# An attention block over 64 sequence pairs on one core: the third pair's keys' product moved between the first pair's probability transposes, a bias fold moved ahead of a turned x1, more warming transposes

## The chip, the cores and the metric

The kernel runs on one core of a Trainium2 chip. The metric is the device time of one execution in microseconds (us), here 1495.01 (median of three runs, 1494.42 to 1495.22). Five engines run side by side, each through a queue of its own in program order: TensorE (PE in the profile; PEld is its weight load) multiplies and transposes into PSUM, VectorE (DVE), ScalarE (ACT) and GpSimd (POOL) do elementwise work and reductions, SyncE (SP) and ScalarE issue transfers. They meet through semaphores.

## The reference

One transformer block with cross attention, float32, over 128 sequences of 128 positions and 256 features, 16 heads of 16 features, and a hidden layer of 1024:

```python
q = (query @ Wq + bq).reshape(b, s, N_HEADS, D_K).transpose(0, 2, 1, 3)
k = (key @ Wk + bk)...
v = (values @ Wv + bv)...
scores = jnp.einsum('bhqd,bhkd->bhqk', q, k) / jnp.sqrt(jnp.float32(D_K))
scores = jnp.where(j < i + mask, scores, NEG_INF)
attn = jax.nn.softmax(scores, axis=-1)
attn = attn.at[:, :, 0, :].set(0.0)
ctx = jnp.einsum('bhqk,bhkd->bhqd', attn, v)...
attn_out = ctx @ Wo + bo
x = layer_norm(query + attn_out, ln1_g, ln1_b)
ffn = jax.nn.relu(x @ W1 + b1) @ W2 + b2
out = layer_norm(x + ffn, ln2_g, ln2_b)
```

Here `mask` is 0 and `key` and `values` are the same context tensor, so that each position sees strictly earlier ones, and position 0 sees none.

## The kernel before

The 128 sequences are taken as 64 pairs (`p`); every function below works on one pair. A pair goes through: `tokens` (its rows, transposed on DVE), `queries`, `keys` and `values` (products on TensorE, copied out of PSUM by ACT), `scores` (TensorE; `hi=1` is the high half of the rows, which sees all 128 columns, `hi=0` the low half, which sees 64), `mask` and `maximum` (DVE, then a subtraction on POOL), `exponential` (ACT), `sums` (DVE, then a division on POOL), a transposition of the probabilities, `weigh` (probabilities by values), `context` (ACT copy), `attention_out`, `attention_sum`, `attention_stats` and `shift` (DVE and POOL), `norm1` (x1), a transposition of x1, `hidden` (first layer, with ACT's ReLU), `second`, the second norm, `store`.

Tile's scheduling is switched off (`manual_schedule`), so the order of the calls is the order of each engine's queue. Pairs 0 to 6 have hand-written orders (the opening in the body, then `third`, `fourth`, `fifth`, `fall_in`, `sixth`); from pair 7 on `step(p)` repeats. In one stage several pairs are under way: `third` takes pair 2 through its scores while pair 0 goes through its first layer and pair 1 through its probabilities.

PSUM is eight banks. Scores use banks 0 to 3. In the opening everything else takes banks 4 to 7 in turn: `bank(name)` raises a counter and returns `4 + turns[0] % 4`. A product may be written to a bank only when the last reader of what it held is done; later stages name fixed banks.

Probabilities of pairs 0 and 1, and x1 of pair 0, are transposed on TensorE (`turn_on_pe`, L493, four 128x128 transposes and an ACT copy for each group; `turn_x1_on_pe`, L710, with ACT's scale and bias at L720). From pair 2 on DVE transposes 32x32 blocks (`turn`, L468) and 16 transfers reorder them (`bring`, L481, from SP's and ACT's queues); x1 takes the same way through DRAM (`turn_x1`, L699: four transfers out at L241, one back at L244).

`keys` is `project_keys` (TensorE, L263) and `copy_keys` (ACT, four copies at L293). `values` is TensorE's product (L303); `values_out` has ACT copy it into two layouts (L317, L326). `fold_values` makes a row that `add_values` (L695) copies to where `add_bo` (POOL, L256) reads it.

`fold_norm1` (L653) multiplies the first norm's bias with W1 on TensorE (L660) and has ACT copy four rows out (L668); `add_b1` (L670) sends them to a column by four transfers. The column is used from pair 1 on.

The program starts with 12 transposes of the identity (L995) whose result nobody reads, before the first context rows have arrived. `hidden` for pair 1 (L738) has empty instructions on TensorE between its products (`empty`, L215): six behind each product of its first group, three behind each of the rest. In the trace each float32 product or projection shows as two instructions.

`load_ahead` and `load_tokens` issue the transfers for later pairs on SP's queue; a transfer may wait for an earlier one of the same semaphore, of which eight are used in turn.

## Time and profile before

| what | us |
| --- | --- |
| median of the runs shown | 1495.01 |
| the profiled execution, whole | 1494.63 |
| its span, first to last instruction | 1492.9 |
| TensorE busy | 1478.8 |
| DVE busy | 1379.4 |
| POOL busy | 1359.7 |
| ACT busy | 1321.3 |

Of the 40 slices of the span, the one that holds the first 37 us has TensorE at eight tenths, all others but the last at nine or more. A row of the timeline has the start in us from the span's beginning, the time that the group took, engine, line, operation, out<-in, shape and count, and in brackets how long the engine had been idle before it and what ended that. Rows of neighbouring instructions of one form are merged, so the time of a group on TensorE includes the drain of its last product; start to start is the better measure there. A matmul's end is modelled.

### The profile page before, as it was taken

Reading aid. Unit: us, or ns where it says so; the run is one execution under the profiler, and the core shown is the slowest. Engines: PE = TensorE matmul, PEld = TensorE weight load, DVE = VectorE, ACT = ScalarE, POOL = GpSimd, SP = SyncE. Lnnn points to the kernel's source line nnn. Section 1 sums busy time; section 2 is a strip of 40 time slices with the busy share of each in tenths; the row PEclk is TensorE's granted clock in tenths of the full one; section 3 lists DMA queues with packets and bytes.
Section 4 is the critical chain, followed back from the end, with each engine's and each line's share of the span. In section 5 each row is a group of like instructions: output and inputs, shape, how many; then the busy total and the mean of one; then the engine's idle time right before and its main releaser. Section 6 shows DMA issues by size and latency. Waiting matters only on the chain.

```text
span 1492.9 us, 53293 instructions
## 1 busy us (share of the span) xinstructions
PE 1478.8 (99%) x19270; PEld 1376.9 (92%) x19270; DVE 1379.4 (92%) x2428; ACT 1321.3 (89%) x5271; POOL 1359.7 (91%) x1510
## 2 busy tenths in 40 slices
PE   8999999999999999999999999999999999999998
PEld 6778999999999999999999999999999999999997
DVE  6989999999999999999999999999999999999965
ACT  5658999999999999999999999999999999999962
POOL 6878899999999999999999999999999999999983
PEclk9999999999999999999999999999999999999999
DMA  9356666566566566556656665666665666664451
GB/s 200 85 109 147 146 146 137 139 143 140 147 139 144 136 141 143 141 132 147 145 135 147 146 136 140 144 138 150 140 143 138 139 140 147 133 143 132 108 126 49
DMA packets 415314, 204.59 MB, mean 137 GB/s; under 512 B 282448, under 2 KB 383056, under 8 KB 415056
## 3 DMA queue, kind: packets, MB, share of 16 engines
q1 hardware_dynamic: 412768, 199.34, 57.5%
q8 instruction: 158, 2.59, 0.8%
q10 hardware_dynamic: 2288, 1.85, 0.5%
q14 instruction: 100, 0.82, 0.2%
HBM read 70.26 MB, written 33.29 MB: 69 GB/s over the span
## 4 chain that ended last, share of the span: by engine, by line
PE 89%; DVE 4%; ACT 3%; POOL 2%; issue 1%; DMA 1%; ACTq 0%; SPq 0%; POOLq 0%; DVEq 0%
PE banks L835 24%; PE banks L933 23%; PE banks L263 14%; PE banks L550 7%; PE banks L303 7%; PE banks L387 6%; PE banks L531 3%; PE banks L521 2%; PE banks L738 2%; ACT sm L800 1%; DVE su L445 1%; PE banks L758 0%; ACT hT L746 0%; DVE sm L411 0%; DVE tb L474 0%
## 5 line engine op out<-in xcount | busy, mean ns | idle before, releaser
L800 ACT ACTIVATE sm<-banks,nmx 128x128 f32<-128x128 f32 x944 | 329.0, 377 | 20.9 <-DVE nmx L784 11.2
L462 POOL TENSOR_TENSOR sm<-sm,rs 128x1024 f32<-128x1024 f32 x171 | 322.3, 1899 | 0.9 <-DVE rs L457 0.9
L800 ACT ACTIVATE sm<-sm,nmx 128x64 f32<-128x64 f32 x944 | 312.3, 365 | 0.0
L474 DVE STREAM_TRANSPOSE tb<-sm 128x1024 f32<-128x1024 f32 x186 | 229.4, 1236 | 12.0 <-DMA pT<-tb 6.9
L964 ACT ACTIVATE hT<-hT,b1e_c 128x256 f32<-128x256 f32 x448 | 191.3, 497 | 28.8 <-DVE hT L952 22.8
L800 ACT ACTIVATION_READ_ACCUMULATOR sm<-sm,nmx 128x1 f32 x912 | 198.9, 218 | 0.0
L800 ACT ACTIVATION_READ_ACCUMULATOR sm<-banks,nmx 128x1 f32 x912 | 197.8, 217 | 0.0
L835 PE MATMUL banks<-wt,hS 128*128 128x128 f32 x1440 | 170.7, 275 | 0.1
L933 PE MATMUL banks<-xS,w1t 128*128 128x128 f32 x1344 | 168.4, 275 | 0.0
L835 PEld LDWEIGHTS banks<-wt,hS 128*128 128x128 f32 x1440 | 165.6, 192 | 0.3 <-DVE hS L820 0.3
L784 DVE TENSOR_REDUCE nmx<-banks 128x4 f32<-128x512 f32 x177 | 153.8, 869 | 6.0
L933 PEld LDWEIGHTS banks<-xS,w1t 128*128 128x128 f32 x1344 | 159.1, 192 | 0.0
L293 ACT ACTIVATE kT<-banks,bkh,half 128x256 f32<-128x256 f32 x252 | 122.0, 584 | 4.0 <-PE banks L263 4.0
L263 PE MATMUL banks<-xT,wq 128*128 128x256 f32 x504 | 125.4, 392 | 0.0
L550 PE MATMUL banks<-wo,cxT 128*128 128x256 f32 x512 | 121.3, 380 | 0.8 <-ACT cxT L543 0.8
L303 PE MATMUL banks<-wv,cT 128*128 128x256 f32 x512 | 120.9, 379 | 0.0
L835 PEld LDWEIGHTS banks<-w,hT 128*128 128x128 f32 x960 | 116.6, 192 | 3.5 <-ACT cxT L543 0.3
L263 PE MATMUL banks<-cT,wk 128*128 128x256 f32 x504 | 119.2, 379 | 0.0
L933 PE MATMUL banks<-x1T,w 128*128 128x128 f32 x896 | 118.3, 275 | 0.0
L835 PE MATMUL banks<-w,hT 128*128 128x128 f32 x960 | 117.5, 275 | 0.1
L550 PEld LDWEIGHTS banks<-wo,cxT 128*128 128x128 f32 x512 | 96.9, 190 | 14.5 <-ACT cxT L543 1.3
L303 PEld LDWEIGHTS banks<-wv,cT 128*128 128x128 f32 x512 | 97.2, 190 | 13.2
(160 smaller groups left out, 3958.4 us busy)
## 6 DMA issues: line engine op xcount, KB each, us to landing
pT<-tb SPq DMA_DIRECT2D x976, 96.0 KB, 2.2
x1t<-tbx SPq DMA_DIRECT2D x252, 64.0 KB, 1.8
x1T<-x1t SPq DMA_DIRECT2D x63, 256.0 KB, 3.0
out_dram<-t SPq DMA_DIRECT2D x63, 256.0 KB, 2.4
xb<-in_x_dram SPq DMA_DIRECT2D x124, 128.0 KB, 4.1
cb<-in_ctx_dram SPq DMA_DIRECT2D x124, 128.0 KB, 3.8
x<-in_x_dram SPq DMA_DIRECT2D x31, 512.0 KB, 4.7
w<-in_L_xattn_W_dram SPq DMA_DIRECT2D x2, 1024.0 KB, 8.2
```

The source lines that it names most:

```text
L263: nc.tensor.matmul(ps[:, m * TP : (m + 1) * TP], w[:, k, m * P : (m + 1) * P], src[:, k, :], start=(k == 0), stop=(k == KC - 1),)
L293: nc.scalar.activation(st["kT"][:, m, e, :], pk[:, m * TP : (m + 1) * TP], AF.Identity, bias=bkh[:, m, e : e + 1], scale=half[:, e : e + 1],)
L303: nc.tensor.matmul(pv[:, s * D : (s + 1) * D], st["cT"][:, k, s * P : (s + 1) * P], wv[:, k, :], start=(k == 0), stop=(k == KC - 1),)
L387: nc.tensor.matmul(st["sps", hi][r][s * HP : (s + 1) * HP, m * 2 * n : (m + 1) * 2 * n].rearrange("p (e j) -> p e j", e=2), st["qT"][strip ...
L462: nc.gpsimd.tensor_tensor(sm[:, part, :], sm[:, part, :], st["rs", hi][:, part, None].to_broadcast([P, part.stop - part.start, sm.shape[2] ...
L474: nc.vector.transpose(st["tb"][:, :, at : at + 256].rearrange("p j (n a) -> p n j a", a=32), st["sm", hi].rearrange("p h j -> p (h j)")[:, ...
L550: nc.tensor.matmul(po[:, s * D : (s + 1) * D], cxT[:, k, s, :], wo[:, k, :], start=(k == 0), stop=(k == KC - 1),)
L784: nc.vector.tensor_reduce(st["nmx", 1][:, 4 * first : 4 * (first + n)], ps, AX.X, ALU.max, negate=True,)
L800: nc.scalar.activation(sm[:, h, :], src, AF.Exp, bias=nmx[:, h : h + 1], scale=1.0, **({"accum_out": st["su", hi][:, h : h + 1]} if summed ...
L835: nc.tensor.matmul(out, left(k), right(k), start=(k == 0), stop=(k == FC // 2 - 1))
L933: nc.tensor.matmul(ps[:, i * P : (i + 1) * P].rearrange("p (n a) -> p n a", a=32), left(i), right, start=True, stop=True,)
L964: nc.scalar.activation(self.hT[:, f], self.plains.get(f, self.hT[:, f]), AF.Relu, bias=b1e_c[:, f : f + 1], scale=1.0,)
```

## The change

The diff touches the opening only; the repeated `step` stays as it is.

```diff
+    def next_bank(i):
+        turns[0] = (i - 5) % 4
...
                     if p == 1:
-                        empty(3 if f else 6)
+                        empty(2)
...
-    for i in range(12):
-        nc.tensor.transpose(warm[:, i % 4 * P : (i % 4 + 1) * P], ident, ident)
+
+    def keep_warm(n):
+        for i in range(n):
+            nc.tensor.transpose(warm[:, i % 4 * P : (i % 4 + 1) * P], ident, ident)
+
+    keep_warm(16)
     states[0] = {}
...
         nc.vector.tensor_copy(st[which + "T"].rearrange("p k i -> p (k i)"), pt)
+    keep_warm(3)
...
     ps_bv = fold_values()
+    add_values(ps_bv)
+    tokens(2, "c")
     sums(0, 0, ALL)
     scores(1, 1)
     mask(1, 1, A)
     maximum(1, 1, ONE)
+    values_out(1)
     turn_on_pe(0, 1, range(2))
-    add_values(ps_bv)
-    values_out(1)
-    turn_on_pe(0, 1, range(2, 4))
+    next_bank(6)
+    project_keys(2)
+    next_bank(5)
+    turn_on_pe(0, 1, range(2, 3))
+    next_bank(7)
+    turn_on_pe(0, 1, range(3, 4))
     mask(1, 1, B)
     maximum(1, 1, TWO)
     add_bo(0)
+    next_bank(4)
     turn_on_pe(0, 0, range(2))
     tokens(2, "x")
     scores(1, 0)
     exponential(1, 1, ONE)
+    next_bank(7)
     weigh(0)
...
     maximum(1, 0, ALL)
-    tokens(2, "c")
     exponential(1, 1, TWO)
...
     shift(0, 1)
+    copy_keys(2)
     exponential(1, 0, ALL)
     sums(1, 1, TWO)
-    keys(2)
     norm1(0)
     sums(1, 0, ALL)
     nc.gpsimd.tensor_tensor(be1b_r, be1_r, b2_r, ALU.add)
+    next_bank(7)
     values(2)
...
         maximum(p, 1, ONE)
+        fold_norm1()
+        add_b1()
         turn_x1_on_pe(0)
         turn_on_pe(1, 1, range(2))
-        fold_norm1()
-        add_b1()
         hidden(0, range(FC // 4))
...
         tokens(3, "c")
-        load_ahead(2)
-        load_tokens(2)
         exponential(p, 0, ALL)
...
         hidden(0, range(3 * FC // 4, FC), lambda f: bring(p, nc.scalar, EVERY[8:]))
+        load_ahead(2)
+        load_tokens(2)
```

In words, with pairs counted from 0: the first warming run has 16 transposes, and three more follow the transposes of the first tokens. ACT copies the folded row and pair 1's values before the first copies of pair 0's turned probabilities. DVE transposes pair 2's context before pair 0's low sums, TensorE makes pair 2's key product between the second and third group of pair 0's high half, and ACT copies these keys before pair 1's low Exp. `next_bank(i)` makes the next `bank` return bank i, so that the rotation fits the new order. In `third`, the bias fold and its four transfers stand before the transposes of pair 0's x1. The loads of pairs 6 and 7 and of the third group of tokens are issued at the end of `third`, behind pair 2's reordering transfers and pair 1's x1. The empty instructions in pair 1's first layer become two behind each product.

## The prediction

> **What bounds the kernel now.** I read the page first, then TensorE's waits over the first 130 us, then the timeline of that stretch engine by engine.

> ```profile
> span 1492.9 us, 53293 instructions
> ...
> PE 1478.8 (99%) x19270; PEld 1376.9 (92%) x19270; DVE 1379.4 (92%) x2428; ACT 1321.3 (89%) x5271; POOL 1359.7 (91%) x1510
> ```

> TensorE is busy throughout. Its waits in the first 130 us (engine, line, releaser: total, times, longest) are:

> ```profile
> PE banks L504 <- ACT vd L326: 2.3, 1, 2.3
> ...
> PE banks L738 <- DMA x1T<-x1t: 0.6, 1, 0.6
> PE banks L387 <- ACT hT L746: 0.6, 1, 0.6
> ```

> From 160 us on the same view has no entry. So the loop over pairs runs at TensorE's pace, and whatever the opening gains or loses by about 95 us is carried to the end one for one. All edits lie in that opening; the sum is the shift of TensorE's timeline there.

> **1. The warming transposes.** TensorE's timeline (start, us, line, count):

> ```profile
> 1.44 2.82 PE L995 MATMUL banks<-ident 128*128 128x128 f32 x12 [1.44 <-POOL ident masks.py:199]
> 4.97 1.12 PE L230 MATMUL banks<-ident,c_first 128*128 128x128 f32 x4 [0.70 <-DMA c_first<-in_ctx_dram]
> 5.88 1.06 PE L230 MATMUL banks<-ident,x 128*128 128x128 f32 x4
> 6.87 3.31 PE L1019 MATMUL banks<-cT,wk 128*128 128x256 f32 x8
> 10.02 1.89 PE L1040 MATMUL banks<-xT,wq 128*128 128x256 f32 x8
> 11.84 1.34 PE L358 MATMUL banks<-kT,qT 32*64 32x256 f32 x32
> 14.04 1.89 PE L303 MATMUL banks<-wv,cT 128*128 128x256 f32 x8
> 15.77 1.89 PE L263 MATMUL banks<-xT,wq 128*128 128x256 f32 x8
> ```

> From start to start a transpose takes 0.23 us at 4.97 (0.91 / 4; 0.12 later, 1.94 / 16 in the row at 28.25 below); a 128x256 instruction takes 0.39 at 6.87 (3.15 / 8), 0.23 at 10.02 (1.82 / 8) and 0.22 at 14.04 (1.73 / 8). So TensorE runs at half speed until about 9.6 us: near the end of L1019. Twelve transposes at 0.23 end near 4.2; four more reach 5.1 at most and fill the wait for c_first, 0.1 us beyond it. Three more behind the x transposes fill the wait for the copy of cT. With both gaps filled, TensorE has no pause of note from 1.44 on. If the clock then opens some 3.4 us sooner, L1019 runs at 0.22: 3.15 - 1.73 = 1.42 us saved, 0.09 more on L1040, less some 0.1 where the three transposes reach past 6.87. I take 1.45 saved. The bounds: 1.9 saved if the clock opens even ahead of 4.97 (four transposes 0.44 sooner), 0.3 lost if it opens no sooner (three cold transposes end at 7.5, 0.6 late, and cold work put off is done at 0.22 instead of 0.39).

> [...]

> ```profile
> 25.00:30.00 5.00, 2.74 (x24) 2.48 (x24) 4.90 (x8) 3.59 (x10) 5.00 (x3) 1.00 1.01 202
> ```

> and in the timeline:

> ```profile
> 24.89 1.09 PE L504 MATMUL banks<-ident,sm 128*128 128x128 f32 x8 [0.43 <-POOL sm L447]
> 28.25 1.94 PE L504 MATMUL banks<-ident,sm 128*128 128x128 f32 x16 [2.26 <-ACT vd L326]
> ```

> From 24.9 to 30.1 TensorE did nothing but transposes and waiting, and the granted clock stayed 1.00 (the 16 took 0.12 each). [...]

> **2. The keys of pair 2 in the stall.** More rows around it:

> ```profile
> 22.94 5.61 POOL L447 TENSOR_TENSOR sm<-sm,rs 128x1024 f32<-128x1024 f32 x3
> 24.11 1.22 DVE L445 TENSOR_REDUCE su<-sm 128x16 f32<-128x1024 f32 x1 [0.42 <-ACT sm L430]
> 26.55 0.39 ACT L695 COPY bov_r<-banks 128x256 f32<-128x256 f32 x1
> 26.81 0.68 ACT L317 COPY vz<-banks 128x256 f32<-128x256 f32 x2
> 27.34 0.77 ACT L326 COPY vd<-banks 64x256 f32<-64x256 f32 x2
> 36.04 1.89 PE L263 MATMUL banks<-cT,wk 128*128 128x256 f32 x8
> 37.97 1.93 ACT L293 ACTIVATE kT<-banks,bkh,half 128x256 f32<-128x256 f32 x4 [1.27 <-PE banks L263]
> 39.46 1.17 DVE L445 TENSOR_REDUCE su<-sm 128x16 f32<-128x1024 f32 x1
> 39.59 1.12 PE L358 MATMUL banks<-kT,qT 32*64 32x256 f32 x32
> ```

> The stall of 2.26 us is bank 5: the third transpose group takes it while ACT still copies values out of it, behind two pT copies. The change lets ACT do those copies (0.39 + 0.68 + 0.77) from 24.1 on, ahead of the pT copies, so bank 5 is free at 25.9. The product (8 x 0.22 = 1.73) runs from 25.8 to 27.5, the two later groups to 28.4. The low half then waits for POOL's third division, done at 22.94 + 5.61 = 28.55, so scores of pair 1 start near 29.5, 0.6 before 30.11. The 1.73 us at 36.04 fall away, so the scores of pair 2 come at 37.3 instead of 39.59: 2.3 us. On DVE the 0.70 us transpose of pair 2's context comes before L445 at 24.11, where 0.42 is idle: 0.28 late until it is skipped at its old place. ACT's key copies (1.93) go ahead of pair 1's low Exp, which would end near 37.7; its sums come on DVE at 38.9 or later (39.46 less 0.6), so 1.2 us of cover hide it; without them DVE would wait the difference. The other banks that the change names are free when taken: pair 2's keys lie in the bank that L695 has read, and the turned groups follow copies that are done. Only the second group of pair 1's high half meets a copy still running, that of pair 2's values (bank 7, read by 41.7 in part 3), and that isn't what ends last there.

> **3. What these 2.3 us buy.** Next comes pair 0's x1. The chain behind it:

> ```profile
> 38.30 0.23 POOL L570 TENSOR_SCALAR ve<-mv 128x2 f32<-128x2 f32 x1 [0.60 <-DVE mv L564]
> 39.78 1.09 ACT L592 ACTIVATE x<-t,nb,sd 128x256 f32<-128x256 f32 x2
> 42.07 1.02 ACT L720 ACTIVATE x1T<-banks,be_c,g_c 128x256 f32<-128x256 f32 x2
> 43.47 1.99 PE L738 MATMUL banks<-x1T,w 128*128 128x256 f32 x8
> 43.93 1.52 ACT L668 COPY early<-banks 1x256 f32<-1x256 f32 x4
> 45.50 0.84 ACT L746 ACTIVATE hT<-banks,b_c 128x256 f32<-128x256 f32 x2
> 46.14 1.42 DVE L411 TENSOR_TENSOR sm<-banks,neg 128x256 f32<-128x256 f32 x4 [0.38 <-PE banks L358]
> 53.34 1.22 DVE L445 TENSOR_REDUCE su<-sm 128x8 f32<-128x1024 f32 x1 [1.93 <-ACT sm L430]
> ```

> POOL waited only 0.60 before L570, so it can start it no more than 0.6 sooner; with the 0.28 of DVE handed through its queue I take 0.4, so x1 starts at 39.38. ACT then has, in order: x1 and the values of pair 2 (42.07 - 39.78 = 2.29), and now, ahead of x1T, the four bias copies L668 (1.52), then x1T (1.02). Together 4.83 (bank 7 is read by 41.7): x1T is there at 44.2 and hidden's first group starts at 44.25, against 43.47. TensorE, early as it is, waits: **+0.75** where the stall promised -2.3. The bias product on TensorE falls into this wait; its four small transfers go into SP's queue about 1 us sooner, past nothing, and their bias is first used by pair 1's ReLUs after 80. Behind the group wait the low scores of pair 2 and DVE's mask, which was already waiting on them (0.38 at 46.14), then the Exp behind which DVE idles 1.93 at 53.34. From there on each step waits for the one before (Exp, DVE's sums, POOL's divisions and norms, the next pair's maxima), so the chain keeps its +0.75 up to 85 us. With the old order x1T would come at 42.7 and TensorE would be free at 42.1, a gain; 0.75 is bounded by these: +0.95 (x1 no sooner than 0.2) and -1.4 (42.05 - 43.47, if x1T is not what TensorE waits for).

> **4. Loads behind pair 2's transposed probabilities, fewer empty instructions.**

> ```profile
> 64.29 6.02 SPq L489 DMA_DIRECT2D pT<-tb  x8
> 79.27 7.46 PE L738 MATMUL banks<-x1T,w 128*128 128x256 f32 x32 [0.58 <-DMA x1T<-x1t]
> 85.05 0.84 ACT L746 ACTIVATE hT<-banks,b1e_c 128x256 f32<-128x256 f32 x2
> 87.66 1.59 PE L387 MATMUL banks<-kT,qT 32*64 32x256 f32 x56 [0.55 <-ACT hT L746]
> 88.50 1.95 DVE L411 TENSOR_TENSOR sm<-banks,neg 128x256 f32<-128x256 f32 x4 [0.44 <-DMA x1t<-tbx]
> ```

> Five load issues leave SP's queue ahead of the eight pT and five x1 transfers and follow them; all stay, so no bytes change. x1T lands sooner, and the 0.58 at 79.27 goes. The empties fall from 60 to 32: 32 x 1.73 / 8 = 6.92 against the row's 7.46, up to 0.5 off. Both end at ACT's last two ReLU pairs (85.05 plus two of 0.84 = 86.73 plus the shift), so the scores can start near 86.8 instead of 87.66; DVE, free at 88.06 (88.50 less 0.44), starts at once instead of waiting. **-0.45** passes, the rest becomes a longer TensorE wait at L758. If the loads come too late for the fifth pair's transposes (first needed after 100 us) this cover is gone, but there are more than 20 us of it.

> **Sum.** -1.45 + 0.75 - 0.45 = -1.15 us. The profiled execution took 1494.63 (span 1492.9 and 1.73 around it), so 1493.5; the median of the runs, 1495.01, stands 0.38 above it, so I forecast **1493.9**.

> **Rivals.** (a) *x1T is not what hidden waits for*, the -1.4 bound: the stall's gain passes. -1.45 - 1.4 - 0.45 = -3.3, so 1491.7. For it speaks the size of the stall, against it ACT's unbroken row from 39.78 to 45.50. (b) *The clock opens no sooner*: +0.3 + 0.75 - 0.45 = +0.6, so 1495.6, **slower**; here the change doesn't warm. It decides as soon as no stretch before 6.87 opens the clock. For it: twelve transposes opened nothing by 4.97. Against it: the gaps of 0.70 and of the cT copy lay between them. [...] (c) *The clock closes in the new wait*: from 39.5 to 44.25 TensorE would have 1.35 us of work. Half speed for one stretch of 3.4 us puts 1.7 us on the chain; with (b) and more of it, +2.3 to +3.5, so about 1497.8. Against it: the 28.25 stall, with 1.1 us of work in 3.4, closed nothing.

> **From this the numbers.** Chances: forecast 0.42, (a) 0.30, (b) 0.20, (c) 0.08. The range reaches from a little below (a), 1491.0, to beyond (b), 1496.2; its own, around the forecast, is 1493.3 to 1494.5. A measurement of this kernel tells about 0.2%, 3.0 us, from no change: faster means under 1492.0, where most of (a) lies (0.25); slower, over 1498.0, half of (c) (0.05); the forecast, (b) and the rest lie within (0.70).

> **What would show it.** Right: L1019's eight at about 0.22; no wait on vd at 28; keys' product at 25.8; hidden's first group waiting on L720, near 42.8 (44.25 less 1.45), bias copies ahead of it; no wait on x1T's transfer; pair 4's scores about 1.15 sooner than 87.66. Step 1 is wrong if L1019 stays at 0.39, step 3 if hidden's first group starts before 42 or waits on something else, step 4 if the wait on x1T's transfer remains.

## The result, and the profile after

The changed kernel takes **1501.19 us** (median of six runs, 1497.87 to 1502.91) against 1495.12 for the kernel before beside it: ratio 1.0042 [1.0032, 1.0052]. It is slower by 0.4%, outside the predicted range. The profiled execution is the fastest of the six, 1497.87 with a span of 1496.1; the kernel before had 1494.63 and 1492.9.

The page of the changed kernel, span, busy times and TensorE's instruction queue:

```profile
span 1496.1 us, 53282 instructions
...
PE 1480.3 (99%) x19277; PEld 1375.2 (92%) x19277; DVE 1380.6 (92%) x2428; ACT 1322.9 (88%) x5271; POOL 1361.2 (91%) x1510
...
q8 instruction: 158, 2.59, 0.8%
```

Its three longest TensorE waits in the first 130 us (releaser: total, times, longest):

```profile
PE banks L266 <- issue: 1.6, 1, 1.6
PE banks L741 <- ACT x1T L723: 1.5, 1, 1.5
PE banks L1000 <- POOL ident masks.py:199: 1.4, 1, 1.4
```

and its timeline (line numbers are three higher than before, L1000 five and L1027 eight):

```profile
1.45 3.38 PE L1000 MATMUL banks<-ident 128*128 128x128 f32 x16 [1.45 <-POOL ident masks.py:199]
4.73 0.66 PE L233 MATMUL banks<-ident,c_first 128*128 128x128 f32 x4
6.17 1.99 PE L1027 MATMUL banks<-cT,wk 128*128 128x256 f32 x8
9.82 1.34 PE L361 MATMUL banks<-kT,qT 32*64 32x256 f32 x32
23.81 1.89 PE L266 MATMUL banks<-cT,wk 128*128 128x256 f32 x8
29.88 0.70 PE L266 MATMUL banks<-xT,wq 128*128 128x256 f32 x2
32.20 1.46 PE L266 MATMUL banks<-xT,wq 128*128 128x256 f32 x6 [1.62 <-issue]
37.03 1.12 PE L361 MATMUL banks<-kT,qT 32*64 32x256 f32 x32
38.92 1.09 ACT L595 ACTIVATE x<-t,nb,sd 128x256 f32<-128x256 f32 x2 [1.56 <-POOL nb L618]
41.22 1.53 ACT L671 COPY early<-banks 1x256 f32<-1x256 f32 x4
42.77 1.02 ACT L723 ACTIVATE x1T<-banks,be_c,g_c 128x256 f32<-128x256 f32 x2
43.39 2.02 PE L741 MATMUL banks<-x1T,w 128*128 128x256 f32 x8 [1.49 <-ACT x1T L723]
86.53 1.59 PE L390 MATMUL banks<-kT,qT 32*64 32x256 f32 x56 [0.28 <-ACT hT L749]
88.22 1.95 DVE L414 TENSOR_TENSOR sm<-banks,neg 128x256 f32<-128x256 f32 x4 [0.29 <-DMA x1t<-tbx]
```

Step by step the opening went much as foreseen, but for its size: the clock is open by the c transposes at 4.73 (four in 0.49 us from start to start), the 2.26 us wait on `vd` is gone, pair 2's scores start 2.56 us sooner (37.03, was 39.59), and the first layer waits for x1T behind the bias copies. New is a pause of 1.62 us inside pair 2's queries that the profile puts down to "issue" alone. At 95 us the changed kernel is 0.27 us ahead (DVE's row at 93.80 of the one, 94.07 of the other), where 1.15 was forecast. At the end it is 3.2 behind: **the loss is in the steps that the diff does not touch**. TensorE's weight loads there (160 to 1440 us), first before, then after:

```profile
PEld banks L263 <- issue: 9.4, 55, 0.2
```

```profile
PEld banks L266 <- issue: 7.4, 43, 0.2
PEld banks L266 <- DVE sm L414: 3.4, 12, 0.3
PEld banks L390 <- issue: 2.2, 5, 0.7
```

L390 is `scores`. One such stretch in the timeline of weight loads, before and after:

```profile
192.14 1.38 PEld L387 LDWEIGHTS banks<-kT,qT 32*64 32x64 f32 x64
193.69 1.59 PEld L263 LDWEIGHTS banks<-xT,wq 128*128 128x128 f32 x8 [0.17 <-issue]
```

```profile
191.91 0.30 PEld L390 LDWEIGHTS banks<-kT,qT 32*64 32x64 f32 x17
192.87 0.94 PEld L390 LDWEIGHTS banks<-kT,qT 32*64 32x64 f32 x47 [0.66 <-issue]
```

Behind the 17th of 64 weight loads TensorE stops, and the profile shows no engine and no transfer of data that it waits for. What falls due there, by an estimate from counts, is its own code. The page's queue q8, of the kind "instruction", makes 158 transfers of 2.59 MB in all: 16.4 KB each. The program before has 40530 TensorE instructions (38540 weight loads and matmuls on the page, the rest semaphore and empty instructions). If these transfers bring them, one has 64 bytes (2.59 MB / 40530) and a transfer holds a **block of 256** (16.4 KB / 64); which instructions a transfer brings, no trace says. Counted in program order as the trace has them (a float32 transposition is two instructions, a product four, an empty one), a repeated step is 640, two and a half blocks. So the scores of the steps start by turns at two *places* within a block: 43 and 171 before. The change takes 28 empties out, adds seven transposes (14) and two semaphore instructions: 12 fewer, places 31 and 159. Place 159 plus 34 instructions (17 weight loads, 17 matmuls) is 193. All five long pauses in `scores` stand at this place, and the pause among the queries is at place 194 of an earlier block. The 28 steps at place 159 hold the whole 3.0 us of the loss: about half inside the scores, half right behind them, where the queries' weight loads now wait for DVE (L414, 12 times, 3.4 us). This is the place theory; its rivals are that the changed order, the clock, or the chip makes the difference. The clock isn't it: from 10 to 1490 us it is granted whole (1.00) in this profile and in that of before.

### The profile page after: what moved, and what is told of

Same layout as the page of the kernel before. It is cut to its first block, busy times and chain, and to the rows that moved or that the text cites. A ratio compares the mean times of both kernels' runs of the same rounds, so it can differ in the third digit from the quotient of the medians.

```text
span 1496.1 us, 53282 instructions
## 1 busy us (share of the span) xinstructions
PE 1480.3 (99%) x19277; PEld 1375.2 (92%) x19277; DVE 1380.6 (92%) x2428; ACT 1322.9 (88%) x5271; POOL 1361.2 (91%) x1510
## 3 DMA queue, kind: packets, MB, share of 16 engines
q8 instruction: 158, 2.59, 0.8%
## 4 chain that ended last, share of the span: by engine, by line
PE 91%; DVE 3%; POOL 2%; ACT 2%; issue 1%; DMA 0%; POOLq 0%; SPq 0%; DVEq 0%; ACTq 0%
PE banks L838 24%; PE banks L936 23%; PE banks L266 14%; PE banks L553 7%; PE banks L306 7%; PE banks L390 6%; PE banks L534 3%; PE banks L524 2%; PE banks L741 2%; DVE su L448 1%; DVE sm L414 1%; ACT hT L749 1%; PE banks L761 0%; DVE tb L477 0%; ACT sm L803 0%
## 5 line engine op out<-in xcount | busy, mean ns | idle before, releaser
L803 ACT ACTIVATION_READ_ACCUMULATOR sm<-sm,nmx 128x1 f32 x912 | 202.1, 222 | 0.0
L266 PEld LDWEIGHTS banks<-xT,wq 128*128 128x128 f32 x504 | 90.7, 189 | 24.0 <-issue 9.5
```

The lines of the kernel that those rows point to most:

```text
L266: nc.tensor.matmul(ps[:, m * TP : (m + 1) * TP], w[:, k, m * P : (m + 1) * P], src[:, k, :], start=(k == 0), stop=(k == KC - 1),)
L803: nc.scalar.activation(sm[:, h, :], src, AF.Exp, bias=nmx[:, h : h + 1], scale=1.0, **({"accum_out": st["su", hi][:, h : h + 1]} if summed ...
```

## The experiments

The ratio behind each time is against the kernel before on the same chip. "Steps" is how much the shift against the profile of before grows from 100 to 1418 us.

**1. The places put back.** The changed kernel with 44 empties in place of 32:

```diff
-                        empty(2)
+                        empty(3 if f else 2)
```

> The whole change, with 12 more empty instructions in pair 1's first layer (2 in its first group, 3 in the rest: 44 instead of 32), so that every later TensorE instruction stands at the same place of its 256-instruction block as in the kernel before (scores of the repeated step at 43 and 171 instead of 31 and 159). Theory (place in the block): the 3 to 6 us are lost in the scores of every second repeated step and go away, while the opening's lead of 0.27 us stays: about 1494.8, and TensorE's weight loads of the scores no longer pause 0.2 to 0.8 us there. Rival (the new order of the opening leaves later stages worse off): stays at 1500 to 1501.

1495.14 us, ratio 1.0007 [0.9998, 1.0016]; steps 0.0. The wait in `scores` is gone, and the row for weight loads is that of the kernel before:

```profile
PEld banks L266 <- issue: 9.4, 55, 0.2
```

Twelve instructions that do nothing, at about 80 us, take back the loss in the 1300 us behind them.

**2. The kernel before at the changed kernel's places**, 48 empties in place of 60:

```diff
-                        empty(3 if f else 6)
+                        empty(3)
```

> The kernel before, with 12 empty instructions fewer in pair 1's first layer (3 behind each product, 48 instead of 60) and nothing else. Theory (place in the block): the repeated steps now stand where the changed kernel's do, so it loses as much: 1498 to 1501, with the same pauses. Rival: 12 empty instructions less change nothing, 1495.

1495.70 us, ratio 1.0008 [0.9999, 1.0017]: the time missed what was expected. The mechanism shows all the same: 0.46 us ahead behind the opening, 2.0 lost in the steps, and in its waits

```profile
PEld banks L387 <- issue: 0.8, 2, 0.4
```

So these places cost some 2 us in this run and 3.0 in the profile of the change: the place says where TensorE may wait, not for how long. By the time alone, with 1 inside the interval, this run doesn't tell the kernel from the one before.

**3. The empties of before in the changed kernel**, 60:

```diff
-                        empty(2)
+                        empty(3 if f else 6)
```

> The whole change but for the empty instructions, which are as before (60): the repeated steps stand at 59 and 187, 16 further than before and 28 further than in the changed kernel. Theory (place in the block): another time than the changed kernel's; the place where the load pauses (192) comes 5 instructions into the scores instead of 33, ahead of their short products, so near 1495, if the next block is there by then; 1498 or more if not. Rival (the order of the opening): 1500 to 1501 as with the change.

1499.43 us, ratio 1.0035 [1.0022, 1.0047]; steps 4.8. The pauses move behind the scores of the other steps (scores are 128 instructions: those that start at 59 end at 187, and place 193 lies six further, in the queries):

```profile
PEld banks L266 <- issue: 17.3, 77, 0.5
```

In this run the clock was also closed for one window (granted 0.94 from 40 to 45 us and 0.72 from 45 to 50, which comes to 3.4 us at half), and the first layer's first group took 3.3 us instead of 1.95 (rival (c) of the prediction); at 95 us it is 1.9 us behind.

**4. The bias fold put back**, on top of the first:

```diff
-        fold_norm1()
-        add_b1()
         turn_x1_on_pe(0)
         turn_on_pe(1, 1, range(2))
+        fold_norm1()
+        add_b1()
```

> As the one with 12 more empties (places 44 and 172), and the bias fold back behind the first turned x1. Theory of the prediction (ACT's four bias copies of 1.5 us ahead of x1T hold hidden's first group): that group starts about 1.2 us sooner than in the one with 12 more empties, and about 1 us of it reaches the end: 1493.8. Rival (the order of the fold costs nothing): the same as that one, about 1494.8.

1495.30 us, ratio 1.0004 [0.9995, 1.0013]. In its profile x1 starts at 38.06 and hidden at 41.74, 3.68 us apart, where the changed kernel has 43.39 - 38.92 = 4.47: the fold ahead of x1T costs 0.79 us there (experiment 1, with the fold ahead, has 4.46 too). The median doesn't show it; runs lie between 1492.75, the profiled one, and 1497.9.

**5. The changed kernel again**, in a later measurement, on another chip than experiments 1 to 4.

> The changed kernel itself, for a comparison on one chip with the three beside it. Place theory (TensorE waits for its instructions at place 192 of a block of 256, which in this kernel lies 33 instructions into the scores of every second step): again slower, 1498 to 1502, with the pauses inside L387/L390. If its earlier 1501 was a matter of the chip or of the hour, it comes out within 1 us of the kernel before.

1497.69 us, ratio 1.0023 [1.0014, 1.0032]: slower again, by less than at first and just under what was expected. At 95 us this profile is 0.98 behind, with a closed window of the clock in the first layer (granted 0.90 from 40 to 45 us, 0.76 from 45 to 50), where the first one was 0.27 ahead. Steps 1.6, with one long pause in `scores` instead of five:

```profile
PEld banks L390 <- issue: 0.4, 1, 0.4
```

**6. The kernel before with 16 more empties**, and nothing else:

```diff
-                        empty(3 if f else 6)
+                        empty(4 if f else 7)
```

> The kernel before with 16 more empty instructions in pair 1's first layer and nothing else, so that the scores of the steps start at places 59 and 187 of a block, as in the run with the changed order and 60 empties (1499.4). Place theory: the opening loses at most 0.5 us, the steps lose about 4.5 us in pauses behind the scores of even steps, 1498.5 to 1500. Rival (the changed order or the clock made that run slow, not the place): 1494.5 to 1495.5.

1499.49 us, ratio 1.0031 [1.0019, 1.0042]; steps 5.4, the opening unchanged in sum (0.01 us at 95 us). This settles place against order: the old order at 59 and 187 loses what the new one does.

```profile
PEld banks L263 <- issue: 17.7, 76, 0.6
```

**7. Thirteen warming transposes and none behind the tokens**, places 43 and 171:

```diff
-                        empty(2)
+                        empty(4 if f else 2)
...
-    keep_warm(16)
+    keep_warm(13)
...
-    keep_warm(3)
```

> The changed kernel at the places of the kernel before (43 and 171), with 13 warming transposes in the first run and none behind the first tokens. If the warming is worth what the trace shows (scores of pair 0 start 2.0 us sooner) and this lasts: the clock opens near 9.6 us, scores of pair 0 start near 11.8, and the run takes 1496.5 to 1497.5, 1.5 to 2 us above the same order with 16 and 3 (1495.1). If the warming is worth nothing at the end because the gained time is waited away behind it: 1494.6 to 1495.6.

1493.98 us, ratio 1.0000 [0.9991, 1.0009]: below the first experiment (on another chip) by more than a microsecond, and below both expectations. Its timeline says why:

```profile
6.76 2.00 PE L1026 MATMUL banks<-cT,wk 128*128 128x256 f32 x8 [0.35 <-DVE cT L1008]
...
30.47 1.99 PE L266 MATMUL banks<-xT,wq 128*128 128x256 f32 x8
32.74 1.89 PE L553 MATMUL banks<-wo,cxT 128*128 128x256 f32 x8 [0.28 <-issue]
...
42.63 3.29 PE L741 MATMUL banks<-x1T,w 128*128 128x256 f32 x8 [1.48 <-ACT x1T L723]
```

The clock was open by 6.76 without the extra transposes (the keys' eight take 1.83 us from start to start, 3.15 before), and with 12 instructions fewer ahead, places 192 to 194 fall on the first attention-out product, where only 0.28 us is lost. The last row is rival (c) again; over that window the trace has (TensorE, PEld, DVE, ACT, POOL busy with counts, clock, DMA share, GB/s):

```profile
43.22:46.63 3.41, 3.41 (x39) 2.37 (x38) 0.98 (x1) 1.45 (x4) 3.26 (x2) 0.50 0.04 1
```

**8. The kernel before with 40 fewer empties** (20 in place of 60, not the 17 of the expectation), places 3 and 131:

```diff
-                        empty(3 if f else 6)
+                        empty(1 if f else 2)
```

> The kernel before with 17 empty instructions in place of 60 in pair 1's first layer, so that the scores start at places 3 and 131 and place 192 lies 61 instructions into the scores of every second step, and as far behind them in the others. Place theory: pauses inside the scores at least as large as those of the changed kernel (0.24 to 0.79 us in every second step), 3 to 10 us in all, less up to 0.4 for the empties: 1497 to 1505. Rival (empties cost time and their place nothing): 1493.8 to 1495.

1496.21 us, ratio 1.0016 [1.0007, 1.0025], steps 1.9: slower, a little below what the theory gave. Pauses don't simply grow with the distance into the scores, as had been assumed: no weight load inside the scores waits longer than 0.1 us. The loss lies right behind those scores that contain place 193, in the queries' wait for DVE, for which the profile of before has no such row:

```profile
PEld banks L263 <- DVE sm L411: 3.2, 9, 0.4
```

In eight of the 28 steps place 193 comes 0.71 to 0.74 us after the first weight load of the scores in place of 0.49, and in just these eight the wait behind the scores is near 0.4.

**9 and 10. Ten transposes in the wait for x1**, on the fourth and on the first experiment, places kept (24 empties). On the fourth:

```diff
+        keep_warm_next(10)
         turn_x1_on_pe(0)
         turn_on_pe(1, 1, range(2))
         fold_norm1()
```

On the first, they stand ahead of `hidden`. `keep_warm_next` writes to the bank that is taken next.

> The changed kernel at the places of the kernel before, the bias fold back behind the turned x1 and probabilities, and ten more transposes of the identity where TensorE waits for x1 (1.4 us in the run with the fold put back; that run took 1492.75 when its clock stayed open and up to 1497.9 in others). If clock closings in that wait spread those runs: the clock stays at 1.00 from its opening to the end, spread under 2 us, 1492.5 to 1493.5, below the kernel before by 1 to 2 us. If the spread has another cause: 1494.5 to 1496 with runs up to 1497 as there.

> The changed kernel at the places of the kernel before, with ten more transposes in the 1.5 us in which TensorE waits for the turned x1 ahead of the first layer. Closing theory: no closed window at 40 to 48 us, first group of the first layer at 1.95 us from start to start, 1494 to 1495 with few runs above. Without closings in play: like the same kernel without them, 1495.1.

1494.75 us, ratio 1.0003 [0.9994, 1.0012], and 1495.71, ratio 1.0012 [1.0003, 1.0021]: neither as expected. The clock closed all the same, earlier: in the profile of the first from 32.9 to 36.3, right behind a pause among pair 2's queries that was longer than any so far (the six behind it take 2.51 us from start to start, 1.29 in the changed kernel):

```profile
33.23 2.72 PE L266 MATMUL banks<-xT,wq 128*128 128x256 f32 x6 [2.18 <-issue]
```

In the second it closes from 33.3 to 36.7, behind a pause of 2.02 us in the same place. So in both a closed window follows this pause, which transposes elsewhere don't fill.

**11. The new warming alone in the kernel before**, 16 and 2, places kept by 12 fewer empties:

```diff
-                        empty(3 if f else 6)
+                        empty(3)
...
+    keep_warm(16)
...
+    keep_warm(2)
```

> The kernel before with the new warming alone (16 transposes and 2 behind the first tokens), places held by 12 fewer empties. If the warming counts by itself: clock open between 4.3 and 7 us in the profile, scores of pair 0 start at 9.8 to 10.5 instead of 11.84; at the end 1.5 us sooner, 1492.5 to 1493.5. If what is gained is given back, because the clock that opens sooner closes for one window in the 2.3 us stall at 24 to 28 us: 1494 to 1495, with a row of clock 0.5 near 27 us.

1494.30 us, ratio 0.9999 [0.9990, 1.0007]. Scores of pair 0 start 1.44 us sooner than in the profile of before, at 10.40, and in the profiled run, the slowest of the eleven, it is given back: the clock closes in the stall on `vd`, for two windows (0.50 for 6.83 us).

```profile
10.40 1.34 PE L358 MATMUL banks<-kT,qT 32*64 32x256 f32 x32
...
26.81 3.65 PE L504 MATMUL banks<-ident,sm 128*128 128x128 f32 x16 [2.26 <-ACT vd L326]
```

```profile
26.00:32.83 6.83, 6.02 (x100) 5.39 (x104) 4.84 (x9) 3.96 (x8) 6.11 (x4) 0.50 0.99 234
```

**12. Experiments 4 and 7 together**: the keys' product moved, places as before (one instruction off), 13 warming transposes, the fold back in its old place.

```diff
-        fold_norm1()
-        add_b1()
         turn_x1_on_pe(0)
         turn_on_pe(1, 1, range(2))
+        fold_norm1()
+        add_b1()
```

> The changed kernel at the places of the kernel before (one instruction off), with 13 warming transposes and none behind the first tokens, and the bias fold back behind the turned x1 and probabilities. Place theory of the opening: place 192 falls on the first products behind pair 3's queries, the pause there is at most 0.3 us as in the run with the fold ahead (1493.98), where the kernels with 14 more instructions paused 1.1 to 2.2 us inside these queries. With the fold back, first norm to first layer takes 3.7 us instead of 4.5: 1492.8 to 1493.8, below the kernel before by 0.5 to 1.5. If the fold's place is worth nothing because TensorE then waits for x1 itself: 1493.8 to 1494.5.

**1493.09 us** (11 runs, 1491.94 to 1494.47) against 1494.45: ratio 0.9990 [0.9981, 0.9999], a little faster than both kernels and as expected, though the pause ahead of attention-out was 0.61 us and not 0.3 at most. x1 to first layer is 41.73 - 38.03 = 3.70 us:

```profile
32.62 1.89 PE L553 MATMUL banks<-wo,cxT 128*128 128x256 f32 x8 [0.61 <-issue]
...
38.03 1.09 ACT L595 ACTIVATE x<-t,nb,sd 128x256 f32<-128x256 f32 x2 [2.32 <-POOL nb L618]
41.73 1.99 PE L741 MATMUL banks<-x1T,w 128*128 128x256 f32 x8
```

All twelve, and the change at its first measurement, sorted by the places at which the scores of the steps start:

| places | kernel | ratio to before | steps, us |
| --- | --- | --- | --- |
| 43/171 | before | 1 | 0 |
| 43/171 | 1, places back | 1.0007 | 0.0 |
| 44/172 | 4, fold back | 1.0004 | 0.0 |
| 43/171 | 7, 13 transposes | 1.0000 | -0.1 |
| 44/172, 43/171 | 9, 10 | 1.0003, 1.0012 | -0.1, -0.1 |
| 43/171 | 11, before with warming | 0.9999 | 0.0 |
| 44/172 | 12, both | 0.9990 | 0.0 |
| 3/131 | 8, before | 1.0016 | 1.9 |
| 31/159 | the change, again | 1.0042, 1.0023 | 3.0, 1.6 |
| 31/159 | 2, before | 1.0008 | 2.0 |
| 59/187 | 3, change | 1.0035 | 4.8 |
| 59/187 | 6, before | 1.0031 | 5.4 |

Old order or new, every profile at 43 or 44 loses nothing in the steps, and every other one does.

## Why the prediction was wrong

**The step that failed** is in its first part: "whatever the opening gains or loses by about 95 us is carried to the end one for one". The diff moved the places of all later instructions by 12, which no term of the sum priced; the empties were costed as time on the spot ("up to 0.5 off"). In the profiled run that cost 3.0 us up to 1418 us, more than the whole opening had gained; it made the sign. None of the rivals was this one. The sum itself failed too: with the places held (experiment 1) the change is no faster than the kernel before, 1.0007 [0.9998, 1.0016], so the 1.15 us aren't there either; the terms below say where they went. In the other runs of the first measurement the loss is up to 5 us more than in the profile. They have no trace. Their mean granted clock is 0.997 to 0.999, the profiled run's 0.999; one window of 3.41 us at half takes 0.001 off that mean (an estimate, 3.41 x 0.5 / 1496) and costs about 1.4 us where a trace shows it, so closed windows may be a part of it. Why the same kernel lost less in experiment 5 stays open.

**Warming (-1.45 predicted).** In the pair of profiles scores of pair 0 start 2.02 us sooner (9.82, was 11.84), a little more than the upper bound of 1.9. Rival (b) is wrong here: the c transposes at 4.73 take 0.12 us each (0.49 / 4), with only transposes ahead of them. No run shows a set 3.4 us by which the clock opens sooner, as the sum has it: granted whole from 9.57 us in the profile of before, it was from 4.38 here, 5.19 sooner, and from 6.85 in experiment 3, 2.72 sooner. And the size was taken from one execution. Of the four profiles with 12 transposes two opened in time (the keys' product L1019 at about 0.23 each, experiments 2 and 6) and two late (before and experiment 8); all with 16, and both with 13, were open. And experiment 11 measures the term alone: nothing in the median. In its profile the clock that opened sooner closed again in the next stall; how often that happens in runs without a trace isn't known. The closed stretches in the traces are 3.41 us long (experiment 7, 43.22 to 46.63; experiment 2, 26.92 to 30.33) or twice that (experiment 11, 6.83).

**The keys in the stall** did what was said: no wait on `vd`, the product at 23.81 (25.8 forecast, less the clock's 2.0), pair 2's scores 2.56 us sooner.

**x1T late (+0.75).** The mechanism was right: hidden waited on x1T with the bias copies ahead of it. x1 to first layer grew from 3.69 to 4.47 us, 0.78. The start, 43.39, is 0.6 later than the 42.8 forecast: x1 came at 38.92 where -1.45 on 39.38 gives 37.93. That is the 1.62 us pause among the queries, through attention-out and the norm: x1 starts 5.43 us behind attention-out's first product here (33.49) and 5.43 and 5.41 behind it in experiments 4 and 12, where the pause was short and x1 came at 38.06 and 38.03. Again the pause stands at such a place (194, by the count), and again the change moved it there: the keys' 16 instructions and 14 of warming lie ahead of it.

**Loads and empties (-0.45).** No wait on x1T's transfer is left at hidden, as foreseen, and pair 4's scores came 1.13 us sooner (1.15 forecast). But DVE's mask only came 0.28 sooner (88.22, was 88.50): it still stood idle 0.29. What it waited for isn't settled; of -1.15 us, -0.27 passed.

**Rival (c)**, given 0.08, is real in the new order: in the profiles of experiments 3, 5 and 7 the clock closes for one window in the first layer, which costs about 1.4 us (3.29 against 1.9 for its first group) where 1.7 was put on the chain. That a stretch lasts 3.4 us no trace of before shows; the one in experiment 7 has 3.41 at 0.50. The argument against it, that the stall at 28.25 closed nothing (granted 1.00 from 25 to 30 us), came from one execution: in the profiles of experiments 2, 6 and 11 a closed clock began in that same stall of 2.26 us or within 0.4 us of its end, for one window, one and two.

## What to carry to other kernels

In this kernel, with TensorE busy 99% of the time, 12 to 40 empty instructions more or fewer at about 80 us moved the places of all later ones and cost 1.9 to 5.4 us in the steps (experiments 2, 6 and 8). So where an engine is as busy, measure an edit with the later places held (by empties) as well as without, before the edit itself is judged. If a profile shows "issue" waits that move when nothing near them was changed, count the instructions between them. And a gain in the first microseconds read from one profile is worth checking in several: with the same 16 transposes the clock opened anywhere from 4.38 us (the change) to 6.85 (experiment 3).

## What the runs showed of the hardware

```
kernel               starts      ends    goes on   later by
the change           29.07       30.64   32.20     1.56
experiment 1         29.17       30.92   32.37     1.45
experiment 3         29.87       31.36   32.76     1.40
experiment 4         28.47       29.98   31.34     1.36
experiment 5         28.64       30.26   31.90     1.64
experiment 7         29.63       31.18   32.74     1.56
experiment 9         30.50       31.69   33.23     1.54
experiment 10        30.19       31.73   33.18     1.45
experiment 12        29.50       31.11   32.62     1.51
```

So TensorE goes on 1.36 to 1.64 us after the transfer, however long it has stood, and that transfer starts anywhere from 28.5 to 30.5; what sets it was not tried. Ahead of it TensorE takes its instructions fast: the scores of a step (64 weight loads in 1.38 us) use code at nine times the rate of the queries' products (46 loads a microsecond against 5, from 8 loads in 1.59 us), and the probabilities' products at twelve times (62, from 32 loads in 0.52 us in the profile of before). That the block's transfer then has too little time is an explanation that fits, not one shown by itself.
